# Three stages in the expert loop, and one PSUM bank for two key products

## The chip, the cores and the metric

The kernel runs on one core of one Trainium2 chip. The metric is device time in microseconds (us) of one execution; the time shown for the kernel is the median of three runs. The engines have short names in the profile: PE is TensorE (matmuls; PEld are its weight loads), DVE is VectorE, ACT is ScalarE, POOL is GpSimd and SP is SyncE, which here does nothing but issue DMAs.

## The reference

Two layers are applied to x of shape (8, 1024, 256), all in float32. The first is an RWKV block: a time mix with a scan along the sequence, then a channel mix. The second, which the change is about, is a mixture of 32 experts of which each token uses four:

```python
# x: 8192 tokens of 256 numbers, normalised
sel_logits = jnp.einsum('nd,ed->ne', xt, expert_sel)          # 32 experts
gates = jax.nn.sigmoid(sel_logits)
sel_val, sel_idx = jax.lax.top_k(gates, N_HEADS)              # 4 of them
...
scores = jax.nn.relu(jnp.einsum('nd,edf->nef', xt, keys))     # 256 -> 128
scores = scores * gate_full[:, :, None]                       # 0 where not chosen
out = jnp.einsum('nef,efv->nv', scores, values)               # 128 -> 256
```

The kernel computes the products for the four chosen experts alone, and multiplies by the gate at the end.

## The kernel before

**Blocks and groups.** The 8192 tokens are 16 blocks of 512. A block goes through the RWKV layer, its four experts per token are found, and its rows are scattered to an array `xs` in HBM, where the rows of one expert lie together. The blocks form three groups of 10, 5 and 1 (numbered 0, 1, 2 in the code; "groups 2 and 3" of the change's title are the code's 1 and 2). When a group's rows are all there, `tile_table` works out which rows and experts its tiles have, and `experts(g, pause)` runs the tiles: 96 in group 0, 56 in group 1, 24 in group 2. Then `combine(g)` gathers each token's four results from the array `ys`, weighs and sums them.

**A tile** is 256 rows of one expert ("whole"), or, for the last 16 tiles of each group, two times 128 rows of two experts ("halves"). It goes through these steps, named by what they write:

- `fetch`: SP brings the rows from `xs` (`xg`); with halves these are two DMAs.
- `turn`: PE transposes the rows, four transposes into one PSUM tile `trx`; `move` copies it to SBUF as `xgT` (L866; on DVE in group 0, on ACT in groups 1 and 2).
- `places`: three small DVE instructions work out where the results go (`later`, `order`, `to`).
- `keys`: DVE copies the expert's key matrix (`key`, L773), one copy for a whole tile, two for halves, from a pool of four buffers.
- `hidden`: PE multiplies keys and `xgT` into a PSUM tile `ph` of 256 columns; ACT applies Relu, giving `hs` (L872).
- `result`: PE multiplies `hs` and the expert's values into `po`; ACT copies that to `yg` (L876).
- `send`: POOL scatters `yg` to `ys` with two indirect DMAs (L822).

**The order.** `experts` unrolls a loop over steps. At step s PE does `result` of tile s-4, `hidden` of tile s-2 and `turn` of tile s, in that order, since `STAGE = 2` lies between a tile's result and its use. ACT then does `xgT` of tile s, `hs` of tile s-2 and `yg` of tile s-4, and DVE does `places` and `keys` of tile s. The helper `pinned` fixes the order of all these on each engine. The helper `after` makes each of the three ACT instructions wait for the last PE instruction of the step, which is the last transpose of `turn` ("one signal for three stages").

**Buffers.** PSUM has two pools of four tiles, `ps_a` and `ps_c`; a tile of either takes one bank[...], also where it is smaller, as `ph` is. `trx` and `ph` come from `ps_a`, `po` from `ps_c`. In SBUF, `xgT` and `hs` have three buffers each. Which buffer a tile gets is settled when the program is built, and each reuse gets a wait for the last reader.

**When.** The loop over blocks runs the streams of the groups beside the blocks, a few steps at each call of `advance`. When the last block is through, `blocks_over` is set, and what is left runs by itself: in the trace this is shortly before PE's `count` matmul (L605, at 1252.40 us), which stands behind the transposes of tile 19 of group 1. From there on some pools of the blocks serve the tiles too (tags `xT`, `k2`, `xn`, `xa`). Group 2 starts its tiles when group 1 has done all of its steps.

Of the kernel before, what the change touches and what calls it, by code (L numbers as in the profile page):

```python
# [8 lines left out]
F32 = mybir.dt.float32  # L9
# [10 lines left out]
P = 128  # L20
# [7 lines left out]
TS = 256  # L28
# [6 lines left out]
def rwkv_then_routed_experts(  # L35
# [22 lines left out]
    KC = D // P  # L58
# [11 lines left out]
    p2 = ctx.enter_context(tc.tile_pool(name="p2", bufs=2))  # L70
    p3 = ctx.enter_context(tc.tile_pool(name="p3", bufs=3))
    p4 = ctx.enter_context(tc.tile_pool(name="p4", bufs=4))
    p16 = ctx.enter_context(tc.tile_pool(name="p16", bufs=16))
    ps_a = ctx.enter_context(tc.tile_pool(name="ps_a", bufs=4, space=PSUM))
    ps_c = ctx.enter_context(tc.tile_pool(name="ps_c", bufs=4, space=PSUM))
# [502 lines left out]
    blocks_over = []  # L578
# [118 lines left out]
    def experts(g, pause):  # L697

        table, limit = tables[g]
        T = n_tiles[g]  # L700
# [6 lines left out]
        def value(t, column, half, engine):  # L707

            start = t - t % RUN if t < whole_only else t - (t - whole_only) % RUN
            if (engine, start, column, half) not in ahead:  # L710
                stop = min(start + RUN, whole_only if t < whole_only else T)
                _, ahead[engine, start, column, half] = nc.values_load_multi_w_load_instructions(
                    table[column + half : column + half + 1, start:stop],
                    engines=[engine],
                    min_val=0,
                    max_val=most[column],
                    skip_runtime_bounds_check_because=WHY,
                )
            return ahead[engine, start, column, half][t - start]

        def parts(t):

            return [(0, 0, SJ)] if t < whole_only else [(j, j, j + 1) for j in range(SJ)]
# [3 lines left out]
        def pinned(ins):  # L727

            before_it = latest.get(ins.ins.engine)
            if before_it is not None:  # L730
                tc.add_manual_dep(
                    ins.ins,
                    before_it,
                    mybir.DependencyInfo(mybir.DependencyClass.NoSync, mybir.DependencyReason.DATA),
                    reason="the tiles keep their order",
                )
            latest[ins.ins.engine] = ins.ins.name
            return ins

        def fetch(t):  # L740
            tag = "xT" if blocks_over and t % 2 else "xg"
            xg = p3.tile([P, SJ, DX], F32, tag=tag, name=f"xg_{g}_{t}")
            for half, j0, j1 in parts(t):
                at = value(t, ROW, half, ET.SP)
                n = j1 - j0
                source = xs[g][bass.ds(at, n * P), :].rearrange("(p j) d -> p j d", j=n)
                nc.sync.dma_start(out=xg[:, j0:j1, :], in_=source)
            return xg

        def places(t, xg):  # L750

            later = p2.tile([P, SJ, TOP], F32, tag="later", name=f"later_{g}_{t}")
            pinned(
                nc.vector.tensor_tensor(
                    later,
                    xg[:, :, D + 1 : D + 1 + TOP],
                    limit[:, :, t : t + 1].to_broadcast([P, SJ, TOP]),
                    ALU.is_gt,
                )
            )  # L760
            order = p2.tile([P, SJ], F32, tag="order", name=f"order_{g}_{t}")
            pinned(nc.vector.tensor_reduce(order, later, AX.X, ALU.add))
            to = p16.tile([P, SJ], U32, tag="to", name=f"to_{g}_{t}")
            pinned(nc.vector.tensor_tensor(to, order, xg[:, :, D], ALU.add))
            return to

        def keys(t):

            ks = []
            for half, _, _ in parts(t):  # L770
                e = value(t, EXPERT, half, ET.DVE)
                key = p4.tile([P, KC * P], F32, tag="key", name=f"key_{g}_{t}_{half}")
                pinned(nc.vector.tensor_copy(key, wexp[:, bass.ds(e, 1), : KC * P]))  # L773
                ks.append(key)
            return ks

        def turn(t, xg):
            ps = ps_a.tile([P, KC, TS], F32, tag="a", name=f"trx_{g}_{t}")
            for c in range(KC):
                for j in range(SJ):  # L780
                    last = pinned(
                        nc.tensor.transpose(  # L782
                            ps[:, c, j * P : (j + 1) * P], xg[:, j, c * P : (c + 1) * P], ident
                        )
                    )
            return ps, last

        def hidden(t, xgT, ks):
            ps = ps_a.tile([P, TS], F32, tag="a", name=f"ph_{g}_{t}")
            for key, (_, j0, j1) in zip(ks, parts(t)):  # L790
                cols = slice(j0 * P, j1 * P)
                for c in range(KC):
                    last = pinned(
                        nc.tensor.matmul(  # L794
                            ps[:, cols],
                            key[:, c * P : (c + 1) * P],
                            xgT[:, c, cols],
                            start=(c == 0),
                            stop=(c == KC - 1),
                        )  # L800
                    )
            return ps, last

        def result(t, hs):
            ps = ps_c.tile([P, SJ, D], F32, tag="c", name=f"po_{g}_{t}")
            for half, j0, j1 in parts(t):
                e = value(t, EXPERT, half, ET.PE)
                for j in range(j0, j1):
                    last = pinned(
                        nc.tensor.matmul(  # L810
                            ps[:, j, :],
                            hs[:, j * P : (j + 1) * P],
                            wexp[:, bass.ds(e, 1), KC * P :],
                            start=True,
                            stop=True,
                        )
                    )
            return ps, last
# [13 lines left out]
        def after(ins, pe):  # L832

            if pinned(ins) and pe is not None:
                tc.add_manual_dep(
                    ins.ins,
                    pe.ins.name,
                    mybir.DependencyInfo(mybir.DependencyClass.Sync, mybir.DependencyReason.DATA),
                    reason="one signal for three stages",
                )  # L840


        fetched, turned, made, ks, to = {}, {}, {}, {}, {}
        STAGE = 2
        coming = 0
        for step in range(T + 2 * STAGE):
            while coming < min(T, step + (5 if blocks_over else 3)):
                fetched[coming] = fetch(coming)
                coming += 1
            if step == 0:  # L850
                for _ in range(pause):
                    yield
            r, h = step - 2 * STAGE, step - STAGE
            signal = None
            if 0 <= r < T:
                po, signal = result(r, made.pop(r))
            if 0 <= h < T:
                ph, signal = hidden(h, turned.pop(h), ks.pop(h))
            if step < T:
                xg = fetched.pop(step)  # L860
                trx, signal = turn(step, xg)
            if step < T:
                xgT = turned[step] = p3.tile([P, KC, TS], F32, tag="xgT", name=f"xgT_{g}_{step}")

                move = nc.scalar.copy if g else nc.vector.tensor_copy
                after(move(xgT, trx), signal)  # L866
                to[step] = places(step, xg)
            if step < T:
                ks[step] = keys(step)
            if 0 <= h < T:  # L870
                hs = made[h] = p3.tile([P, TS], F32, tag="hs", name=f"hs_{g}_{h}")
                after(nc.scalar.activation(hs, ph, AF.Relu), signal)  # L872
            if 0 <= r < T:
                tag = "k2" if blocks_over and r % 2 else "yg"
                yg = p3.tile([P, SJ, D], F32, tag=tag, name=f"yg_{g}_{r}")
                after(nc.scalar.copy(yg, po), signal)  # L876
                send(yg, to.pop(r))
            yield
# [248 lines left out]
```

## Time and profile before

| what | value |
|---|---|
| median of 3 runs | 1509.58 us (1509.09 to 1513.51) |
| the profiled execution, whole | 1503.84 us |
| its span, first to last instruction | 1502.1 us |
| PE busy | 1300.0 us (87% of the span) |
| DVE busy | 1014.6 us (68%) |
| POOL busy | 673.5 us (45%) |
| ACT busy | 577.1 us (38%) |
| granted clock of TensorE, mean | 0.946 |

The stretches in which the tiles of groups 1 and 2 run are these (busy time of each engine, in us):

| from to (us) | what runs | PE | DVE | ACT | POOL | DMA share |
|---|---|---|---|---|---|---|
| 1190 to 1222 | first tiles of group 1, last block | 28.78 | 16.30 | 15.70 | 11.95 | 0.71 |
| 1222 to 1284 | table of group 2, last scatters of x | 34.47 | 26.92 | 16.02 | 40.25 | 0.63 |
| 1284 to 1340 | whole tiles of group 1 | 45.79 | 24.01 | 24.29 | 34.96 | 0.82 |
| 1340 to 1390 | halves of group 1 | 35.52 | 26.19 | 19.34 | 29.94 | 0.79 |
| 1390 to 1430 | start of group 2 | 29.99 | 17.22 | 14.91 | 22.16 | 0.60 |
| 1430 to 1487 | halves of group 2 | 37.62 | 36.78 | 21.13 | 36.80 | 0.79 |
| 1487 to 1502 | last sums, output | 0.00 | 7.22 | 0.00 | 0.00 | 0.50 |

"Busy" counts an engine's own work; waiting, register loads and the issue of DMAs are not in it, but for POOL's indirect DMAs, which are. A line of the profile names the engine, the line of the kernel, the operation, and what it writes and reads (`xgT<-trx` is the copy of `trx` to `xgT`); in brackets stand the idle time before it and what ended it. "remote" stands for an end that the profile could not assign to an instruction.

### The profile page before, as it was taken

The numbers are of one execution on the slowest core, as the hardware profiler recorded it, in microseconds if no ns is written. First come the engines' busy times: TensorE is split into PE (matmuls) and PEld (weight loads), VectorE is DVE, ScalarE is ACT, GpSimd is POOL, SyncE is SP. The second block draws the span as 40 slices with busy tenths as digits, with TensorE's granted clock in tenths as the row PEclk, the third lists the DMA queues.
The fourth block names the chain that finished last, engine by engine and source line by source line (L and its number), as shares of the span: only waits on it lengthen the run. The fifth ranks groups of instructions, "written<-read, shape, count | busy, mean of one in ns | idle before, by whom it ended". The sixth has DMA issues, their size and how long they took to land.

```text
span 1502.1 us, 19816 instructions
## 1 busy us (share of the span) xinstructions
PE 1300.0 (87%) x5590; PEld 930.1 (62%) x5590; DVE 1014.6 (68%) x3452; ACT 577.1 (38%) x1122; POOL 673.5 (45%) x688
## 2 busy tenths in 40 slices
PE   5899999998998998959999999999997484787772
PEld 2566666656666666635777777776765373666662
DVE  5758887887886886847566667665576653355474
ACT  3354444443443453423443334333433241443431
POOL 2112245035045035070566566665553466566554
PEclk9999999999999999979999999999998697899897
DMA  9960132132122022031455455544257675788685
GB/s 323 342 217 15 65 128 84 65 127 90 60 72 79 15 72 79 15 108 52 137 157 175 139 146 165 157 143 127 88 165 249 203 245 206 239 251 264 184 282 209
DMA packets 134077, 223.09 MB, mean 149 GB/s; under 512 B 19231, under 2 KB 92229, under 8 KB 133456
## 3 DMA queue, kind: packets, MB, share of 16 engines
q1 hardware_dynamic: 102736, 151.96, 33.2%
q0 software_dynamic: 29184, 68.25, 12.4%
q10 hardware_dynamic: 2048, 1.61, 0.3%
q8 instruction: 46, 0.75, 0.2%
q14 instruction: 63, 0.52, 0.1%
HBM read 110.01 MB, written 124.28 MB: 156 GB/s over the span
## 4 chain that ended last, share of the span: by engine, by line
PE 68%; DVE 10%; issue 8%; another core or an unknown queue 6%; DMA 4%; ACT 2%; POOL 1%; SPq 1%; DVEq 0%; ACTq 0%; POOLq 0%
PE pj_f L245 13%; PE cm L414 13%; PE ph L794 8%; PE po L810 8%; PE trx L782 5%; PE rec L388 3%; PE tm L333 3%; PE pj_r L245 3%; PE pj_w L245 3%; PE pj_v L245 3%; PE pj_k L245 2%; PE lg L460 2%; DMA g<-ys 2%; DVE ac L905 2%
## 5 line engine op out<-in xcount | busy, mean ns | idle before, releaser
L822 POOL DMA_INDIRECT ys<-yg,to x352 | 351.3, 998 | 264.1 <-ACT yg L876 152.0
L554 POOL DMA_INDIRECT xs<-x,row x256 | 254.9, 996 | 104.2 <-issue 69.2
L414 PE MATMUL cm<-wval,k 128*128 128x256 f32 x1024 | 241.4, 380 | 9.2 <-issue 7.8
L414 PEld LDWEIGHTS cm<-wval,k 128*128 128x128 f32 x1024 | 194.6, 191 | 84.0 <-issue 57.8
L245 PE MATMUL pj_f<-xT,wkey 128*128 128x512 f32 x512 | 243.9, 598 | 2.9 <-DVE xa L341 1.8
L810 PE MATMUL po<-wexp,hs 128*128 x704 | 194.6, 400 | 40.1 <-ACT hs L872 25.5
L794 PE MATMUL ph<-xgT,key 128*128 128x256 f32 (+1 forms) x896 | 194.9, 351 | 8.9 <-issue 7.5
L794 PEld LDWEIGHTS ph<-xgT,key 128*128 128x128 f32 x896 | 155.6, 202 | 31.1 <-issue 12.3
L810 PEld LDWEIGHTS po<-wexp,hs 128*128 128x128 f32 x704 | 128.9, 200 | 64.0 <-ACT hs L872 28.5
L905 DVE SCALAR_TENSOR_TENSOR ac<-g,gate,ac 128x256 f32<-128x256 f32 x256 | 123.3, 487 | 61.5 <-DMA g<-ys 40.6
L362 POOL TENSOR_TENSOR x<-x,xa 128x1024 f32<-128x1024 f32 x16 | 38.0, 2375 | 277.0 <-issue 189.2
L406 ACT ACTIVATE k<-pj_f 128x512 f32<-128x512 f32 x128 | 76.5, 598 | 193.7 <-PE pj_f L245 182.9
L782 PE MATMUL trx<-ident,xg 128*128 128x128 f32 x704 | 112.8, 286 | 31.9 <-ACT xgT L866 18.3
L872 ACT ACTIVATE hs<-ph 128x256 f32<-128x256 f32 x176 | 68.5, 389 | 182.4 <-PE trx L782 97.0
L245 PEld LDWEIGHTS pj_f<-xT,wkey 128*128 128x128 f32 x512 | 92.9, 191 | 72.6 <-issue 65.5
L782 PEld LDWEIGHTS trx<-ident,xg 128*128 128x128 f32 x704 | 90.8, 148 | 51.5 <-ACT xgT L866 20.5
L866 DVE COPY xgT<-trx 128x512 f32<-128x512 f32 x96 | 65.5, 682 | 84.5 <-PE trx L782 49.0
L773 DVE COPY key<-wexp 128x256 f32 x224 | 69.1, 318 | 77.7 <-PE ph L794 34.6
L866 ACT COPY xgT<-trx 128x512 f32<-128x512 f32 x80 | 47.1, 589 | 191.3 <-remote 79.1
L322 DVE RECIPROCAL rw<-rw 128x512 f32<-128x512 f32 x32 | 107.3, 3352 | 1.0
L876 ACT COPY yg<-po 128x512 f32<-128x512 f32 x176 | 103.4, 588 | 3.9 <-DMA ys<-yg,to 2.1
L407 ACT ACTIVATE k<-k 128x512 f32<-128x512 f32 x128 | 80.7, 630 | 4.1
(173 smaller groups left out, 1793.9 us busy)
## 6 DMA issues: line engine op xcount, KB each, us to landing
xg<-xs SPq DMA_DIRECT2D x128, 264.0 KB
g<-ys SPq DMA_DIRECT2D x64, 512.0 KB
xs<-zeros SPq DMA_DIRECT2D x6, 4224.0 KB
xg<-xs SPq DMA_DIRECT2D x96, 132.0 KB
x<-in_x SPq DMA_DIRECT2D x16, 512.0 KB
acc<-x SPq DMA_DIRECT2D x16, 512.0 KB
wexp<-in_w_exp SPq DMA_DIRECT2D x4, 2048.0 KB
ac<-acc SPq DMA_DIRECT2D x16, 512.0 KB
```

Of the source, the lines that this page charges most:

```text
L245: nc.tensor.matmul(ps, w(c), rhs[:, c, :], start=(c == 0), stop=(c == KC - 1))
L322: nc.vector.reciprocal(rc, rc)
L407: nc.scalar.activation(k2, k2, AF.Square)
L414: nc.tensor.matmul(m["cm"][t // 2][:, t % 2, :], k2[:, t * P : (t + 1) * P], wval[:, f, :], start=(f == 0 and t % 2 == 0), stop=(f == FC - 1),
L554: s = nc.gpsimd.indirect_dma_start(out=xs[g], out_offset=bass.IndirectOffsetOnAxis(ap=m["row"][:, t, k : k + 1], axis=0), in_=m["x3"][:, t ...
L782: nc.tensor.transpose(ps[:, c, j * P : (j + 1) * P], xg[:, j, c * P : (c + 1) * P], ident)
L794: nc.tensor.matmul(ps[:, cols], key[:, c * P : (c + 1) * P], xgT[:, c, cols], start=(c == 0), stop=(c == KC - 1),)
L810: nc.tensor.matmul(ps[:, j, :], hs[:, j * P : (j + 1) * P], wexp[:, bass.ds(e, 1), KC * P :], start=True, stop=True,)
L822: s = nc.gpsimd.indirect_dma_start(out=ys[g], out_offset=bass.IndirectOffsetOnAxis(ap=to[:, j : j + 1], axis=0), in_=yg[:, j, :], in_offse ...
L866: after(move(xgT, trx), signal)
L876: after(nc.scalar.copy(yg, po), signal)
L905: nc.vector.scalar_tensor_tensor(ac, gk, routed[i][:, t, k : k + 1], ac, ALU.mult, ALU.add)
```

## The change

It changes `experts` alone, and acts on groups 1 and 2.

- `STAGE` becomes 3 for `g > 0`. At step s PE now does `result` of tile s-6, `hidden` of tile s-3 and `turn` of tile s; the loop has T + 6 steps for T tiles instead of T + 4.
- `keys` of a tile moves one step back, so that it is still two steps ahead of `hidden`: at step s DVE does `places` of tile s and then `keys` of tile s-1.
- Once `blocks_over` is set, two neighbouring tiles share one PSUM tile for `ph`: an even tile takes a new one and writes its first half, the next odd tile writes the second half. These tiles come in turns from `ps_a` and from `ps_c`.
- Once `blocks_over` is set, every second `xgT` and `hs` takes a buffer of the blocks' tags `ek` and `ev` (two buffers each), so that there are five of each.

```diff
         def hidden(t, xgT, ks):
-            ps = ps_a.tile([P, TS], F32, tag="a", name=f"ph_{g}_{t}")
+            if not blocks_over:
+                ps = ps_a.tile([P, TS], F32, tag="a", name=f"ph_{g}_{t}")
+            elif t % 2 and pairs:
+                ps = pairs.pop()
+            else:
+
+                pool, tag = (ps_a, "a") if t % 4 < 2 else (ps_c, "c")
+                pair = pool.tile([P, 2, TS], F32, tag=tag, name=f"ph_{g}_{t}")
+                ps = pair[:, 0, :]
+                pairs[:] = [pair[:, 1, :]]
...
-        STAGE = 2
+
+        STAGE = 3 if g else 2
...
-                xgT = turned[step] = p3.tile([P, KC, TS], F32, tag="xgT", name=f"xgT_{g}_{step}")
+                pool, tag = (p2, "ek") if blocks_over and step % 2 else (p3, "xgT")
+                xgT = turned[step] = pool.tile([P, KC, TS], F32, tag=tag, name=f"xgT_{g}_{step}")
...
-            if step < T:
-                ks[step] = keys(step)
+            if 0 <= step - STAGE + 2 < T:
+                ks[step - STAGE + 2] = keys(step - STAGE + 2)
             if 0 <= h < T:
-                hs = made[h] = p3.tile([P, TS], F32, tag="hs", name=f"hs_{g}_{h}")
+                pool, tag = (p2, "ev") if blocks_over and h % 2 else (p3, "hs")
+                hs = made[h] = pool.tile([P, TS], F32, tag=tag, name=f"hs_{g}_{h}")
```

More of the change, by code (lines that the diff above doesn't have):

```diff
@@ L802, in hidden @@
             return ps, last
+        pairs = []
         def result(t, hs):
```

## The prediction

> **What bounds the kernel now.** The page comes first. PE is busy for 87% of the span, but its digits fall at the end: the last ten slices (37.6 us each, from 1127 us on) read 7484787772, where before they are nearly all 9s. The change acts only there.
>
> ```profile
> PE   5899999998998998959999999999997484787772
> POOL 2112245035045035070566566665553466566554
> L822 POOL DMA_INDIRECT ys<-yg,to x352 | 351.3, 998 | 264.1 <-ACT yg L876 152.0
> L866 ACT COPY xgT<-trx 128x512 f32<-128x512 f32 x80 | 47.1, 589 | 191.3 <-remote 79.1
> ```
>
> The second view is the list of waits between 1190 and 1490 us, where the tiles of groups 1 and 2 run (engine, line, released by: us in total, times, longest).
>
> ```profile
> ACT xgT L866 <- remote: 79.1, 16, 14.8
> ACT xgT L866 <- PE trx L782: 77.2, 34, 23.0
> POOL ys L822 <- ACT yg L876: 76.6, 26, 17.8
> DVE key L773 <- PE ph L794: 34.6, 21, 4.0
> PE po L810 <- ACT hs L872: 23.4, 10, 4.7
> PE trx L782 <- ACT xgT L866: 18.3, 7, 4.3
> ```
>
> Everybody waits for everybody: no engine is full. To see why, I read ten microseconds of the halves of group 1, engine by engine (start, duration; in brackets idle time before and its end).
>
> ```profile
> 1354.63 0.66 PE L782 MATMUL trx<-ident,xg 128*128 128x128 f32 x4 [3.35 <-ACT xgT L866]
> ...
> 1359.11 0.66 PE L782 MATMUL trx<-ident,xg 128*128 128x128 f32 x4
> ...
> 1364.88 0.66 PE L782 MATMUL trx<-ident,xg 128*128 128x128 f32 x4 [3.36 <-ACT xgT L866]
> ```
>
> ```profile
> 1353.99 0.59 ACT L866 COPY xgT<-trx 128x512 f32<-128x512 f32 x1 [4.48 <-remote]
> 1354.48 0.39 ACT L872 ACTIVATE hs<-ph 128x256 f32<-128x256 f32 x1
> 1354.75 0.59 ACT L876 COPY yg<-po 128x512 f32<-128x512 f32 x1
> 1355.38 0.59 ACT L866 COPY xgT<-trx 128x512 f32<-128x512 f32 x1
> ...
> 1364.24 0.59 ACT L866 COPY xgT<-trx 128x512 f32<-128x512 f32 x1 [4.42 <-remote]
> ```
>
> ```profile
> 1355.62 1.14 POOL L822 DMA_INDIRECT ys<-yg,to  x1 [2.75 <-ACT yg L876]
> ...
> 1362.32 0.97 POOL L822 DMA_INDIRECT ys<-yg,to  x1 [0.31 <-issue]
> 1365.87 1.02 POOL L822 DMA_INDIRECT ys<-yg,to  x1 [2.58 <-ACT yg L876]
> ```
>
> The transposes at 1359.11 are over at 1359.77, yet ACT's copy of them starts at 1364.24, from 4.42 us of idleness. ACT waits for PE's counter; by the trace's times of that counter, it stepped at 1358.39, 1361.30, 1362.74 and 1364.17, then twice within 0.15 us. So PE's work is done and told late. The late stretch coincides with POOL's six indirect DMAs (1355.62 to 1363.29), and the backlog is told 0.9 us after the last. Over the whole trace this holds: where a wait for PE ended and POOL had issued nothing in the 2.5 us before, PE's word came 0.01 to 0.09 us late on average (144 waits); where POOL had issued for over 60% of that time, 1.3 to 1.8 us (246 waits).
>
> That is a circle: POOL scatters, PE's words are held up, ACT starves, POOL runs out, the words come, and all starts again. One turn is 1353.99 to 1364.24 = 10.25 us for the three tiles that ACT copies in it. A tile costs POOL 2 x 1.28 = 2.56 us (issue to issue, 1359.76 to 1361.04) and PE 2.2 us (one transpose to the next without a wait, 1354.63 to 1356.88). Measured from transpose to transpose, halves take 3.25 us in group 1 (1336.28 to 1385.06, 15 tiles), 3.33 in group 2 (1418.66 to 1468.66), and whole tiles 3.13 (1286.20 to 1336.28, 16 tiles).
>
> A rule of the Trainium skill denies the cause: SBUF — State Buffer, "Who interferes with whom", says that PE and ACT never wait for anyone, as GpSimd shares ports only with VectorE. By the rule a tile would cost POOL's 2.56 us, and deeper staging could win 0.7 us x 60 tiles = 42 us. The rows decide: 3.3 us, in step with POOL's bursts. How POOL holds up PE's word they don't show.
>
> **The change, part by part.** Nothing is computed more or less: PE, ACT, POOL and SP issue the same instructions.
>
> *Three stages, five buffers.* `po` of a step needs an `hs` that ACT made three steps ago, not two. This would let PE run one step further while its words are late. But in the halves `keys` still has four buffers, two a tile, so DVE's copy for a tile waits for `hidden` two tiles earlier, and that is two steps before its own, as now.
>
> *The shared bank.* Here a rule speaks against the change. PSUM — Partial Sum Buffer, "PSUM bank collisions raise a hardware error", asks that PSUM be guarded by bank and not by address: PE must not write one half of a bank while ACT reads the other. If the build keeps that, `hidden` of an odd tile waits until ACT has made `hs` of the even tile, in the step just before. Nearest row: PE's `trx` waiting for ACT's `xgT` of the step before, 18.3 us in 7 waits (2.6 each). Without the guard the part costs nothing, and the one step more might gain; with it PE, at every second tile, is tied to ACT at one step's distance, where `po` is at two now. I take the rule, as the collision would be an error.
>
> One turn then, for halves, counted from the moment the words come; PE stands before an odd tile's `hidden`, one step waits for ACT. ACT: `xgT` 0, `hs` 0.48 to 0.87, `yg` 0.75 to 1.34 (the rows above). PE goes on at 0.9: `ph` to 1.8, `trx` to 2.3, next `po` (0.87) to 3.1, `ph` (0.9) to 4.0, `trx` to 4.5, `po` to 5.3, then stands before the next odd tile. POOL starts at 1.6 with one tile (to 4.2). The first `trx` is told on time, since in the rows the delay begins some 1.4 us after POOL's start; ACT's step runs 2.4 to 3.7, and POOL's second tile to 6.7. From 3.0 on each PE group is told 1.44 us after the last (1361.30, 1362.74, 1364.17): half of `ph` 4.5, other half 5.9, `trx` 7.4, when POOL has just stopped. Two tiles in 7.4 us: 3.7 us a tile. The same count for now's order gives three tiles in 9.8 to 10.2 us, which is what the rows show. For whole tiles `ph` is one group: 6.0 us for two, 3.0 a tile, against 3.13.
>
> Sum: 32 halves (16 a group) x (3.7 - 3.29, the mean of 3.25 and 3.33) = +13 us. Whole tiles behind the blocks, 16 of group 1 at the measured pace, x -0.13 = -2 us; the others I leave at nothing. The part's two ends: if the guard never ends a wait last, halves run at the 3.0 of whole tiles, 32 x (3.0 - 3.29) = -9 us. If each of the 30 odd tiles among the 60 pays the row's 2.6 us with nothing to cover it, +78 us; but PE stands idle for part of that time today, so the range does not go there.
>
> *Two steps more a group.* At the end each step costs 2.2 to 4.0 us (`po` of the last tiles: 1466.90, 1469.09, 1473.06, 1475.97, 1478.21), two of them 5.6; POOL's backlog covers 2.6 (last `yg` ends 1481.89, its scatter starts at 1484.47): +3. Between the groups POOL is idle from 1403.7 to 1412.0, and group 2's first scatter comes two filling steps later, each `trx` and `ph`, 0.44 + 0.87: +2.6. At the start of group 1 the blocks' matmuls fill PE (28.78 of 32 us): nothing; without that cover 2 x 2.2 = 4.4. Together +5.6, between 0 and 12.
>
> *Moved `keys`.* One DVE copy (0.29 us, two for halves) goes behind the next tile's `places`, which waits for its `xg`. Behind it DVE holds the sums of `combine`; `hidden` needs it two steps later, as now. `fetch` is issued as far ahead as now (five). POOL's and SP's queues keep their order. Nothing, at most 15.8 us (DVE's waits for `xg` in this stretch, 8) should they now hold up `keys`; they are long past when `hidden` comes, so 0.
>
> Total +13 - 2 + 5.6 = +16.6 us on the profiled 1503.84 us (span 1502.1 and 1.74 around it), 1520. That execution lies 5.74 us below the median shown; the same sum on the median gives 1526.
>
> **Rivals.** (1) *The third stage wins.* ACT makes `hs` early enough and each turn takes four tiles: (4 x 2.56 + 2.6 of idle POOL) / 4 = 3.2 us or less down to 3.0, 0.1 to 0.3 us for each of 60 tiles, -6 to -18, less some of the steps: about 1500. For it: POOL idles 76.6 us waiting for `yg`. Against: the guard. (2) *POOL and DMA set the pace anyway*: DMA share 0.79 to 0.82 and POOL at 1.28 us an issue; then only the ends of the groups show, 1511. Against: POOL is idle 40% of the halves of group 1 (29.94 busy of 50; with 0.30 between issues still a quarter). (3) *The guard costs whole tiles too*, slower still: 0.5 to 0.8 us for all 60, plus 5.6: 1545 to 1560. It decides if POOL's bursts are so long that even the first `trx` of a turn is told late. That the pairing is never used is excluded by the code: all tiles from about 20 of group 1 on take it.
>
> **Numbers.** Forecast 0.50, (1) 0.22, (2) 0.12, (3) 0.16. The forecast's own range is 1514 to 1540. For 8 of 10 the range reaches over most of (1) and into (3): 1495 to 1550. A difference below 0.3% (4.5 us) can't be told from none here. Faster 0.22; same 0.11, most of (2); slower 0.67.
>
> **What would show it.** Right: PE's `ph` waiting for ACT's `hs` as a new row, turns of two tiles in the halves near 7.4 us, whole tiles near 3.0, `po` hardly waiting. Wrong: no wait of `ph` for `hs`; POOL's wait for `yg` well under 76.6 us; halves at or below 3.2 us. I am wrong as a whole if PE's words come on time in the changed kernel, or the last scatter comes before 1486.

## The result and the profile after

The changed kernel is slower: 1521.59 us, median of 20 runs (1511.15 to 1531.44), against 1513.03 for the kernel before in 20 runs (1505.15 to 1517.02). The ratio is 1.006, with a 95% interval of 1.0043 to 1.0077. The difference of the medians is 8.6 us, where the forecast had 16.6.

From the page of the changed kernel: busy tenths of PE and POOL in 40 slices of 38.0 us, and the group of the scatters (busy us, mean ns, idle us before).

```profile
PE   5899999998998998968999999999988474877681
POOL 2112245035035035070665666666653366655464
L833 POOL DMA_INDIRECT ys<-yg,to x352 | 352.4, 1001 | 271.3 <-ACT yg L890 166.1
```

PE's digits still fall at the end, and POOL stands a little longer for `yg`: 166.1 us, from 152.0. Nothing has been freed. The waits of the last part, 1190 to 1500 us (engine, line, released by: us in total, times, longest), say what replaced what:

```profile
POOL ys L833 <- ACT yg L890: 86.3, 34, 20.6
ACT xgT L879 <- PE trx L782: 71.3, 31, 23.1
...
DVE key L773 <- PE ph L803: 46.2, 41, 3.1
...
PE ph L803 <- ACT hs L886: 29.1, 13, 3.8
...
PE ph L803 <- issue: 24.8, 10, 7.8
...
PE trx L782 <- ACT xgT L879: 13.5, 1, 13.5
```

The row `ph <- hs` did not exist before: PE, about to write the second half of a bank, waits for the Relu that reads the first. Most of the row below it (2.4 us in 3 waits before) is the same wait, as its times show: of PE's 26 waits before `ph` from the first tile of group 1 on, 23, with 47.0 us in all, end 0.05 us after a Relu; of the 3 before, none does. In exchange `po <- hs` (23.4 us before) is gone, and `trx <- xgT` (18.3 us in 7 waits) is down to one wait. PE's waits for ACT have moved to another place.

Two turns of the halves of group 1, ACT first, then PE, then POOL (start, duration; in brackets the idle time before and its end):

```profile
1363.75 0.59 ACT L879 COPY xgT<-trx 128x512 f32<-128x512 f32 x1 [1.21 <-PE ph L803]
...
1367.17 0.59 ACT L879 COPY xgT<-trx 128x512 f32<-128x512 f32 x1 [2.06 <-PE trx L782]
...
1369.72 0.59 ACT L879 COPY xgT<-trx 128x512 f32<-128x512 f32 x1 [1.21 <-PE ph L803]
...
1374.62 0.59 ACT L879 COPY xgT<-trx 128x512 f32<-128x512 f32 x1 [3.55 <-remote]
...
1377.18 0.59 ACT L879 COPY xgT<-trx 128x512 f32<-128x512 f32 x1 [1.21 <-PE ph L803]
```

```profile
1368.09 1.16 PE L803 MATMUL ph<-xgT,key 128*128 128x128 f32 x8 [1.32 <-issue]
...
1371.28 0.60 PE L782 MATMUL trx<-ident,xg 128*128 128x128 f32 x4
...
1375.55 1.16 PE L803 MATMUL ph<-xgT,key 128*128 128x128 f32 x8 [2.80 <-ACT hs L886]
```

```profile
1372.63 0.98 POOL L833 DMA_INDIRECT ys<-yg,to  x1 [0.30 <-issue]
1376.25 0.97 POOL L833 DMA_INDIRECT ys<-yg,to  x1 [2.64 <-ACT yg L890]
```

ACT now works in pairs of tiles. The transposes at 1371.28 end at 1371.88, their copy starts at 1374.62, one microsecond after POOL's last scatter ends (1373.61): PE's word is late as it was before, and the guarded `ph` at 1375.55 stands behind it. But the turns of two tiles are not all alike: 1363.75 to 1369.72 is 5.97 us, 1369.72 to 1377.18 is 7.46.

Where the time went, stage by stage, from the starts of the transposes in the two profiled executions (1503.84 and 1521.02 us):

| stage | before, us | change, us | difference |
|---|---|---|---|
| start to first tile of group 1 (nothing of the change acts) | 1191.1 | 1196.9 | +5.8 |
| tiles 0 to 24 of group 1 | 95.1 | 93.5 | -1.6 |
| tiles 24 to 40, whole | 50.1 | 51.4 | +1.3 |
| tiles 40 to 55, halves | 48.8 | 49.9 | +1.1 |
| last tile of group 1 to tile 8 of group 2 | 33.6 | 37.8 | +4.2 |
| tiles 8 to 23 of group 2, halves | 50.0 | 50.4 | +0.4 |
| last tile to the last scatter | 17.1 | 21.5 | +4.4 |
| from there to the end | 16.4 | 17.8 | +1.4 |

Without the first row, on which nothing of the change acts, 11.4 us are left (the rows are rounded), and three quarters of them lie where the groups fill and drain. That is one pair of executions, and the one before was quick: 1503.84 us, under the 1505.15 to 1517.02 of the 20 runs.

### The profile page after: what moved, and what is told of

Its sections match the earlier page's. It is cut to its first block, busy times and chain, and to the rows that moved or that the text cites. A ratio compares the mean times of both kernels' runs of the same rounds, so it can differ in the third digit from the quotient of the medians.

```text
span 1519.3 us, 19857 instructions
## 1 busy us (share of the span) xinstructions
PE 1310.5 (86%) x5590; PEld 934.1 (61%) x5590; DVE 1015.7 (67%) x3452; ACT 578.5 (38%) x1122; POOL 675.1 (44%) x688
## 5 line engine op out<-in xcount | busy, mean ns | idle before, releaser
L833 POOL DMA_INDIRECT ys<-yg,to x352 | 352.4, 1001 | 271.3 <-ACT yg L890 166.1
L803 PE MATMUL ph<-xgT,key 128*128 128x256 f32 (+1 forms) x896 | 199.9, 357 | 65.9 <-ACT hs L886 29.1
L245 PE MATMUL pj_f<-xT,wkey 128*128 128x512 f32 x512 | 244.6, 600 | 2.6 <-DVE xa L341 1.9
L821 PE MATMUL po<-wexp,hs 128*128 x704 | 188.5, 392 | 4.7 <-issue 2.1
L245 PEld LDWEIGHTS pj_f<-xT,wkey 128*128 128x128 f32 x512 | 93.2, 192 | 72.4 <-issue 65.5
```

The lines of the kernel that those rows point to most:

```text
L245: nc.tensor.matmul(ps, w(c), rhs[:, c, :], start=(c == 0), stop=(c == KC - 1))
L803: nc.tensor.matmul(ps[:, cols], key[:, c * P : (c + 1) * P], xgT[:, c, cols], start=(c == 0), stop=(c == KC - 1),)
L821: nc.tensor.matmul(ps[:, j, :], hs[:, j * P : (j + 1) * P], wexp[:, bass.ds(e, 1), KC * P :], start=True, stop=True,)
L833: s = nc.gpsimd.indirect_dma_start(out=ys[g], out_offset=bass.IndirectOffsetOnAxis(ap=to[:, j : j + 1], axis=0), in_=yg[:, j, :], in_offse ...
```

## The experiments

Single executions of one kernel spread over up to 29 us on the first chip (1500.52 to 1529.43), so sizes are taken from the ratios and places from the profiles. The four sets of runs fell on four chips; the first of these is like that of the first comparison, and the other three turned out to differ from it, so each kernel is compared only with the kernel before on its own chip.

| run | what it is | before there, us | ratio, 95% interval |
|---|---|---|---|
| own_bank | three stages, no shared bank | 1515.65 | 1.0021, 1.0002 to 1.0040 |
| pairs_two | shared bank, two stages | 1515.65 | 1.0035, 1.0013 to 1.0058 |
| only_g1 | three stages in group 1, pairs in both | 1515.65 | 1.0030, 1.0008 to 1.0051 |
| only_g2 | three stages in group 2, pairs in both | 1515.65 | 1.0054, 1.0034 to 1.0074 |
| far_pairs | bank shared by tiles t and t+2 | 1390.26 | 1.0064, 1.0051 to 1.0078 |
| more_keys | the change with more key buffers | 1390.26 | 0.9984, 0.9974 to 0.9994 |
| quiet_two | before, plain stores | 1390.26 | 1.0039, 1.0022 to 1.0057 |
| quiet_three | change, plain stores | 1390.26 | 1.0032, 1.0013 to 1.0050 |
| change_again | the change | 1391.23 | 0.9992, 0.9983 to 1.0001 |
| keys_three | more_keys again | 1391.23 | 0.9969, 0.9956 to 0.9981 |
| keys_two | before with more key buffers | 1391.23 | 0.9955, 0.9942 to 0.9969 |
| keys_quiet | keys_two, plain stores in group 2 | 1392.51 | 1.0088, 1.0059 to 1.0117 |

### Parts of the change alone

**own_bank** keeps the third stage and the five buffers and drops the pairs:

```diff
-            if not blocks_over:
+            if True:
                 ps = ps_a.tile([P, TS], F32, tag="a", name=f"ph_{g}_{t}")
-            elif t % 2 and pairs:
-                ps = pairs.pop()
...
```

> Three stages and five buffers stay, but every key product has a PSUM bank of its own, as before. Theory A (the cost is the two more steps at both ends of each group; POOL and PE's late words pace the tiles in either order): still 6 to 10 us over the kernel before, like the change. Theory B (the cost is the guard on the shared bank: the odd tile's product waits for ACT's hs of the even one): it goes away, -8 to +2 us against the kernel before, the halves at 3.0 to 3.2 us a tile.

**pairs_two** keeps the pairs and goes back to two stages:

```diff
-        STAGE = 3 if g else 2
+        STAGE = 2
```

> Two stages as before, but two key products share a bank, and the five buffers stay. Theory A: within 3 us of the kernel before, the ends of the groups as before. Theory B: 5 to 10 us over the kernel before, with PE's ph waiting for ACT's hs and halves of 3.4 us a tile or more.

**only_g1** and **only_g2** put the third stage into one group each:

```diff
-        STAGE = 3 if g else 2
+        STAGE = 3 if g == 1 else 2
```

> Three stages in group 1 alone; pairs in both groups. Theory A: +3 to +5 us against the kernel before, all of it between the last tile of group 1 and the first of group 2. Theory B: +7 to +10 us, since the pairs are in both groups.

> Three stages in group 2 alone; pairs in both groups. Theory A: +3 to +6 us against the kernel before, at the end (last transpose to last scatter 21 us against 17) and in filling group 2. Theory B: +7 to +10 us, as the pairs are in both groups.

Both theories named a part of it, and neither the whole. The third stage alone gives 1.0021, the pairs alone 1.0035; together that is 1.0056, and the change had 1.006. In us of 1515.65 the parts are 3.2 and 5.3. The smaller part is hardly clear of none: the medians, 1517.98 and 1515.65 us, give 1.0015. The mean granted clock of the runs is 0.941 before, 0.939 in own_bank and 0.939 to 0.940 in the other three. In the trace it is also low where PE does nothing (0.50 from 1330 us on in quiet_two below), so whether the clock has a share in so small a cost is not told apart.

The waits of 1284 to 1500 us show that the guard comes with the pairs. In pairs_two it is there at two stages too:

```profile
PEld ph L803 <- ACT hs L886: 24.5, 12, 5.0
...
PE ph L803 <- ACT hs L886: 18.9, 5, 4.6
...
PE po L821 <- ACT hs L886: 10.3, 7, 3.8
```

Counted as above, 13 of its 14 waits before `ph`, with 42.3 us, end just after a Relu. In own_bank none of 11 does; these are all of the waits of PE itself at that line in the same stretch:

```profile
PE ph L795 <- DVE key L773: 9.6, 3, 5.0
PE ph L795 <- issue: 7.5, 3, 6.5
...
PE ph L795 <- ACT xgT L871: 4.2, 3, 2.0
```

The same stages as above (us), sorted by what each run had there:

| stage | two stages, own banks (before) | three, own banks (own_bank) | two, pairs | three, pairs |
|---|---|---|---|---|
| 16 whole tiles | 50.1 | 49.7 | 54.9, 52.4 | 51.4, 51.5 |
| 15 halves, group 1 | 48.8 | 51.8 | 49.3, 55.1 | 49.9, 50.2 |
| 15 halves, group 2 | 50.0 | 47.2 | 53.6, 52.9 | 50.4, 51.2 |
| last tile of group 1 to tile 8 of 2 | 33.6 | 35.9 | 28.3, 30.5 | 37.8, 39.7 |
| last tile to last scatter | 17.1 | 24.9 | 14.1, 17.2 | 21.5, 21.4 |

(The pair columns hold pairs_two, the change and the two one-group runs, each where its group belongs; the fourth row goes by the depth of group 1.) Read along the first three rows: with own banks the third stage changes nothing (148.9 and 148.7 in sum). Pairs at two stages cost about 10 (means 53.7, 52.2, 53.3), at three only 3 to 4 (51.5, 50.1, 50.8). In these executions the third stage hides most of a guard that would not be there without the pairs. In the last two rows it costs about 7 us each in the mean of the columns, with own banks 2.3 and 7.8: two more steps between the last transpose of a group and its last result. At the end POOL has what is still in flight before it, and the change's scatters from 1484.17 to 1500.17 us come 2.6 to 2.8 us a tile without a pause for the tiles 17 to 23. These stages are single executions, and their sum is larger than the ratios allow (own_bank's rows add up to 10 us over before, its ratio to 3.2); at most the order of the columns is shown. By the ratios the pairs cost 5.3 us at two stages and, as 1.006 less 1.0021, 5.9 at three, so the hiding isn't shown by them.

That the guard makes the cost of the pairs is read from the waits. The pairs bring something else besides, the turns of `ph` through `ps_c`, and no run on this chip has the one without the other.

### Who makes PE's word late

**quiet_two** and **quiet_three** store the results without POOL, at fixed rows in place of those that `to` names, in the kernel before and in the change:

```diff
-                s = nc.gpsimd.indirect_dma_start(
...
+                row = (t % n_tiles_fit) * TS + j * P
+                s = nc.sync.dma_start(out=ys[g][row : row + P, :], in_=yg[:, j, :])
```

> The kernel before, but the results of a tile are stored by SP with two plain DMAs of the same size in place of POOL's two indirect ones; they go to fixed rows, so the sums of combine add other rows than the reference's. Theory A (POOL's indirect DMAs hold up PE's word): in groups 1 and 2 the words come on time (ACT's copy of trx starts within 0.1 to 0.3 us of the last transpose) and a tile takes 2.2 to 2.7 us: 25 to 50 us less than the kernel before. Rival (the traffic of the stores holds it up, whoever issues them): the words stay 1 to 3 us late and a tile at 3.1 to 3.4 us, within 10 us of the kernel before.

> The same replacement in the changed kernel (sums of other rows again). Theory A: words on time, the guard waits little since ACT follows at once: within 10 us of the kernel with two stages and plain stores, two more steps at each end of 2.4 us, thus 0 to 10 us slower than that. Rival (traffic): turns of two tiles stay, 3.3 us a tile.

The tiles did as Theory A says (halves of group 1 at 2.59 and 2.39 us, ACT's copy 0.09 us behind the transposes), and the time did not: what the tiles gain, the sums of `combine` lose behind them. Windows of quiet_two, the tiles and what follows them (busy us of PE, PEld, DVE, ACT and POOL, granted clock, DMA share, GB/s):

```profile
1187.00:1330.00 143.00, 131.63 (x817) 118.23 (x815) 69.51 (x306) 78.60 (x174) 0.00 (x0) 0.98 0.90 277
1330.00:1390.00 60.00, 0.00 (x0) 0.00 (x0) 43.89 (x96) 0.00 (x0) 0.00 (x0) 0.50 0.91 330
```

PE is done 60 us before the end, all 96 sums of DVE there belong to `combine`, and the DMA engines are busy for 0.91 of it. But the test is void for its question, as the chip it fell on has no late words, with POOL busy or not. Counted from 120 us on: of the steps of PE's counter before which POOL's indirect DMAs had filled over 60% of 2.5 us, how many came more than 0.1 us after the last end of a PE instruction that steps it? 45% of 206 in the kernel before, 41% of 205 in the change, 41% of 198 in own_bank, 40% of 203 in pairs_two; and in the later runs none of 503 (change_again), of 487 (keys_two), of 479 (far_pairs). With POOL quiet in those 2.5 us it is 2 to 6% in the four first. **keys_quiet** was to repeat the test beside a group with POOL's stores:

```diff
+            if g == 2:
...
+                    s = nc.sync.dma_start(out=ys[g][row : row + P, :], in_=yg[:, j, :])
```

> The kernel before with more key buffers in the halves, and in group 2 alone the results are stored by SP's plain DMAs at fixed rows in place of POOL's scatter (so the last sums add other rows than the reference's). It decides only on a chip on which PE's words are late in group 1. There, if POOL's indirect DMAs hold them up: late by 1 to 2 us on average in group 1 while POOL issues, within 0.1 us in group 2, where a tile takes 2.2 to 2.7 us in place of 3.3. If the traffic does it: late in group 2 as well, 3.1 us a tile or more. In group 1 the halves take 3.0 us or less if the key buffers matter under late words, 3.2 to 3.3 if not. On a chip with words on time nothing of this is told apart.

It met the last of its cases: none of 441 late. So that POOL's indirect DMAs cause the lateness, on a chip that has it, was not tested. It stands on the coincidence in time, and a second condition that differs from chip to chip is needed besides.

### The change on a chip with words on time

**change_again**, **keys_three** and **keys_two** ran on one chip. The last two take buffers that the blocks no longer need for the second key of a tile of halves:

```diff
-                key = p4.tile([P, KC * P], F32, tag="key", name=f"key_{g}_{t}_{half}")
+                pool, tag = (p2, ("sg", "x3")[t % 2]) if blocks_over and half else (p4, "key")
+                key = pool.tile([P, KC * P], F32, tag=tag, name=f"key_{g}_{t}_{half}")
```

> The change itself, beside the two kernels with more key buffers. Theory A+B (pairs and stages cost some 0.35 and 0.2 per cent by themselves): 1.004 to 1.008 of the kernel before. Theory C (what is lost is lost because DVE, which works in order, stands before a key copy whose buffer PE has not released): the same here, and gone with more key buffers.

> The change with more key buffers in the halves, as in more_keys, beside the change on the same chip. Theory C: 0.5 per cent or more under the change, and at or under the kernel before. Theory A+B: within 0.2 per cent of the change.

> The kernel before with the same key buffers for its halves, nothing else. If the key buffers alone are what helps: at or under the time of the change with more key buffers, 0.995 to 0.999 of the kernel before. If the third stage brings something once the keys are free: 0.2 per cent or more over the change with more key buffers, and 0.999 to 1.001 of the kernel before.

There the change makes no difference (0.9992); both theories had foretold a cost. ACT and POOL of change_again in the halves of group 1:

```profile
1263.57 0.59 ACT L879 COPY xgT<-trx 128x512 f32<-128x512 f32 x1 [1.21 <-PE trx L782]
...
1265.82 0.59 ACT L879 COPY xgT<-trx 128x512 f32<-128x512 f32 x1 [0.90 <-PE trx L782]
```

```profile
1262.96 0.97 POOL L833 DMA_INDIRECT ys<-yg,to  x1 [0.30 <-issue]
1264.24 0.97 POOL L833 DMA_INDIRECT ys<-yg,to  x1 [0.31 <-ACT xgT L879]
1265.52 0.98 POOL L833 DMA_INDIRECT ys<-yg,to  x1 [0.30 <-issue]
1266.80 0.97 POOL L833 DMA_INDIRECT ys<-yg,to  x1 [0.30 <-ACT hs L886]
```

The transposes of these tiles end at 1263.53 and 1265.73: the copies follow after 0.04 and 0.09 us while POOL issues without a pause, every 1.28 us. The tile costs POOL's two issues: the scatters of tiles 40 to 55 start at 1264.24 and 1302.64, 2.56 us a tile. And the guard hardly costs anything. Its row between 1184 and 1370 us:

```profile
PE ph L803 <- ACT hs L886: 18.0, 18, 11.7
```

Of the 18.0 us one wait takes 11.7, and the other 17 take 0.4 us each; on the first chip the 13 waits of this row took 2.2 each.

More key buffers help both orders, and the shallow one more: keys_two, at 1385.05 us, beats the kernel before (1391.23) and the change (1390.13). The same window of change_again, keys_three and keys_two shows what they do, in the fifth pair of numbers, POOL:

```profile
1290.00:1340.00 50.00, 41.37 (x232) 34.27 (x232) 27.66 (x101) 22.67 (x50) 35.91 (x37) 0.92 0.67 220
```

```profile
1290.00:1340.00 50.00, 47.81 (x279) 40.12 (x278) 32.02 (x125) 24.86 (x56) 38.17 (x39) 0.92 0.76 253
```

```profile
1290.00:1340.00 50.00, 41.44 (x247) 35.93 (x247) 30.53 (x114) 22.93 (x52) 38.41 (x38) 0.93 0.74 249
```

50 us hold 39 issues of 1.28, so with more key buffers POOL is full from the end of group 1 into the halves of group 2, and without them it misses two. The 15 halves of group 2 take 35.9 us in keys_three and 43.1 in change_again. How the buffers do it isn't shown: between 1300 and 1350 us DVE stands only 0.4 us for a key's buffer in change_again, and from 1184 to 1370 us about as long with them as without (34.2 us in 20 waits, 34.7 in 25). keys_three, 0.23% under the change, lies between what the two theories gave it. That three stages cost 0.14% once the keys are free (0.9969 against 0.9955, with intervals that overlap) is in line with the drain: last transpose to last scatter 23.7 us in keys_three, 18.1 in keys_two. On the first chip keys_two was not tried; nor was, on any, the start of group 2 while group 1 drains, which would lay the two ends over each other.

**more_keys** was the first of these runs, on another chip, together with **far_pairs**:

```diff
-            elif t % 2 and pairs:
-                ps = pairs.pop()
+            elif t in pairs:
+                ps = pairs.pop(t)
...
-                pairs[:] = [pair[:, 1, :]]
+                pairs[t + 2] = pair[:, 1, :]
```

> The changed kernel, but tiles t and t+2 share a bank, not t and t+1, so the second product of a bank waits for an hs of two steps before. If the guard costs by its distance of one step: as with own banks, 2 to 5 us over the kernel before, no wait of ph for hs. If the sharing costs for another reason (fewer banks, the pools' turns): as the change, 7 to 11 us over.

> The changed kernel with the second key copy of the halves in two tags of the blocks, so that the halves' keys have as many buffers as tiles in flight. If DVE's copies waiting for ph (46 us in the change against 35 before) hold up PE: 2 to 6 us less than the change. If they are a wait off the path: within 2 us of the change, 7 to 11 us over the kernel before.

far_pairs is 8.5 us over the kernel before, like the second of its cases, but not for that reason, as on chips of this kind the change itself costs nothing. The guard is gone from it (none of its 8 waits before `ph` follows a Relu), and yet it is slower. Its halves of group 2 take 50.7 us for 15 tiles, against 43.1 in change_again on another such chip. Between 1300 and 1350 us PE stands before `ph` for DVE's `key` and `later` for 10.3 us, against 4.8 in change_again. The longest of these waits, DVE first, then PE:

```profile
1309.53 2.05 DVE L919 SCALAR_TENSOR_TENSOR ac<-g,gate,ac 128x256 f32<-128x256 f32 x4 [10.78 <-DMA g<-ys]
1311.49 0.29 DVE L773 COPY key<-wexp 128x256 f32 x1
```

```profile
1311.92 1.35 PE L803 MATMUL ph<-xgT,key 128*128 128x256 f32 x4 [4.18 <-DVE later L754]
```

DVE stands 10.78 us for a gather of `combine`, adds, and only then copies the key for which PE stands. Why this order waits longer at such places is open, and on the first chip, where the guard costs, far_pairs was not run. more_keys came out under the kernel before (0.9984). Its expectation was in terms of the change, which did not run on that chip; keys_three beside the change (0.9969 against 0.9992) gives 3 us, within the 2 to 6 expected if the copies hold up PE.

## Why the prediction was right, and where it was off

**The guard: right.** It is in the build, and it is where the prediction put it. As the rule from the Trainium skill had it (PSUM — Partial Sum Buffer, "PSUM bank collisions raise a hardware error"), the second half of a bank waits for the reader of the first: 47.0 us of a new wait (29.1 in the profile's own row), and none with own banks.

**Its size: too large, and this is the term that failed.** "32 halves (16 a group) x (3.7 - 3.29 ...) = +13 us" came to +1.5 for the 30 tiles measured: 3.32 us in group 1 (49.87 / 15) and 3.36 in group 2 (50.38 / 15). The walk through a turn, 7.4 us for two tiles, is met to 0.1 by 1369.72 to 1377.18. The mistake was to take every turn for that one: the turn before takes 5.97, near the 6.0 that the walk gave to two whole tiles. By the ratio the pairs cost 5.3 us alone, or 1.006 less 1.0021, some 5.9, beside three stages, against 11 foretold (+13 and the -2 of whole tiles). The whole tiles didn't gain: 3.21 us, not 3.0.

**The two steps more a group: right in kind.** Forecast +5.6; in the pair of profiles 4.2 between the groups and 4.4 at the end; by own_bank's ratio 3.2, hardly clear of none, with all that the third stage may bring. The end was taken at +3, since POOL's backlog was thought to cover 2.6 of 5.6. It covered less, as POOL has what is left in front of it: 4.4 here, 7.8 in own_bank.

**Moved keys, at nothing: not told apart.** They are within own_bank's 3.2 us. That four key buffers bind the halves was written down, but not priced: where the words come on time, more of them are worth 0.45% in the kernel before.

**The total: luck.** 1520 lies within 2 us of the measured 1521.59, but the forecast difference was 16.6 us and the measured one 8.6. The 8 us too much, some 5 of them in the guard, were offset by the base: the sum stood on an execution of 1503.84 us, 9 us under the later median of 1513.03. On that median the same sum gives 1530.

**The rivals.** (1) The third stage doesn't win: with own banks the tiles' pace stays, 148.7 us against 148.9. (3) Whole tiles lose 0.08 us each, not 0.5. (2) POOL's pace is what rules the halves of group 1 on the other chips, where the time doesn't change (0.9992); its 1511 doesn't follow from its own term, as +5.6 is 1509.4 on the profiled execution and 1515.2 on the median shown. There the number by the rule of the Trainium skill (SBUF — State Buffer, "Who interferes with whom") is met as well: 2.56 us a tile. On the chip of the first profile it isn't, at 3.3. So the mechanism, late words, fits the chip whose trace it was read from, and is not found on every chip.

## What to carry to other kernels

A deeper pipeline has a fixed price, its added steps at each fill and each drain (here some 3 us for two groups by the ratio, hardly clear of none, and more in single executions), so ask for each group of tiles what the depth wins in the middle: here it was nothing with own banks, and with shared ones at most part of the guard that the same change had brought. Two neighbours in one PSUM bank tie the second writer to the first reader at one step's distance, which was nearly free where signals came at once (0.4 us a wait) and came with a cost of 0.35% where they came late. Before adding stages, count the buffers of each operand through all of them: the keys had four, two a tile, and where signals came at once more of them were worth 0.45%, the stage nothing.

## What the runs showed of the hardware

Chips differ. The kernel before took 1513 to 1516 us on the chips of the first comparison and of the first experiments, and 1390 to 1393 on three others, 8% less. The change was profiled on both kinds, with spans of 1519.3 and 1387.8 us. An indirect scatter of POOL takes 1001 ns in both, a matmul of the channel mix (L245) 600 and 598 ns. PE's busy time is 1310.5 and 1265.9 us, at a mean granted clock of 0.935 and 0.969, so about a third of the difference is in PE's own work and the rest in its waits; whether the clock is a cause or falls because PE stands is not told apart. What differs besides is how late PE's words come while POOL issues indirect DMAs: 40 to 45% of the counter's steps come late on the one, none on the others. The first tile of group 1 starts at 1118 to 1123 us there, against 1191 to 1203, so most of the difference arises before the part that the change touches. What in the chip makes it was not found.
